# A graph-attention front in two parts: statistics of 8 tiles first, the next pair of tiles turned ahead, later edge searches moved into the first layer

## The chip, the cores and the metric

The kernel runs on one core of one Trainium2 chip. The core has five engines that run their own instruction streams and meet only at semaphores: TensorE (PE, matrix products; its weight loads are listed as PEld), VectorE (DVE), ScalarE (ACT), GpSimd (POOL) and SyncE (SP, which here only issues DMAs). The metric is the device time of one execution in microseconds (us), lower is better.

## The reference

Four blocks follow each other over 3125 nodes of 256 features, each added to x; the change touches the start of the first one.

```python
def _gat_layer(x, src, dst, W, al, ar, b, n_nodes):
    h = x @ W
    el = h @ al
    er = h @ ar
    e = jax.nn.leaky_relu(el[src] + er[dst], NEG_SLOPE)
    m = jax.ops.segment_max(e, dst, num_segments=n_nodes)
    ex = jnp.exp(e - m[dst])
    s = jax.ops.segment_sum(ex, dst, num_segments=n_nodes)
    alpha = ex / s[dst]
    out = jax.ops.segment_sum(alpha[:, None] * h[src], dst, num_segments=n_nodes)
    return out + b
...
x = x + _L0_gnn_ref(_layernorm(x), src, dst, ...)     # three such layers
x = x + _L0_ffn_ref(_layernorm(x)[None], ...)[0]      # 16 experts, 2 per node
x = x + _L1_gnn_ref(_layernorm(x), W, M, src, dst)    # relu(x@W + sum over edges of x@M)
x = x + _L1_ffn_ref(_layernorm(x)[None], ...)[0]      # 8 experts, 1 per node
```

There are 103125 edges, and the list is sorted by dst. A layer norm (mean and variance of each node's 256 features) stands ahead of the first layer.

## The kernel before

Nodes lie in 25 tiles of 128 rows (NT = 25; the last has 53). The three attention layers work on dense blocks: a count of edges for every pair of a source node and a destination node is made once, kept in SBUF as bytes (counts), and used by all layers. Destinations are taken in 13 groups of two tiles (GROUPS; the last has one).

**The front** (L984 to L1042) runs before the first layer. `load_nodes` brings x in six DMAs of 512 KB and a small one, on SP's queue. `Locator` then brings the whole list dst (whole, on ACT's queue), and copies both lists into DRAM tensors with a tail (dst_p, src_p, L1304 to L1306). `attention_weights` brings W with two extra columns (we), al and ar spread over all partitions (wa) and b (wb), and DVE makes the extra columns, W times al and W times ar, in four products (L923). `locator.find(j)` finds where the edges of part j start: DVE compares every 25th entry of dst with 98 window numbers (less, L1330), PE sums the columns in 33 small matmuls (L1336), DVE turns the sums into row numbers (at, L1338), and POOL gathers 98 rows of 400 edges from either list with indirect DMAs (L1340). There are four parts of 98 windows of 8 destinations. `locator.finish(j)` (L1352) makes the low bits and keys of these edges, with six transposes on PE and copies on ACT.

`Counter` makes the counts of 16 destinations at a time, a pair of windows; a group has 16 pairs, and there are 196 pairs. `make(pair, act)` compares iotas with the edges' low bits and keys on DVE (ohs and ohk, both L1405; with act = 2 two of the six ohs come from ACT by way of far, L1401 and L1402). `add` multiplies them in six matmuls on PE (acc_c, L1417) and ACT writes the sums to counts as bytes (L1420).

The statistics of all 25 tiles (L1009 and L1010), one Sqrt (L1014) and a reciprocal come first, with `finish(0)` between them in the text. Then comes a loop over the groups. It makes two pairs of group 0 and, for either tile, scales x to y (DVE for the first tile L1027, ACT for the second L1030), transposes y on PE (turned, L1033) and copies it to yT (L1035). `Sources.put` (L954) then multiplies yT by we in ps_m (L961), limits the two scores (lr, L964), takes two Exps (L965 and L966) and writes h (L968). Then the two pairs are added; behind groups 1 to 3 stands `find(1)` to `find(3)`.

**A layer** (L1044 on) takes the 13 groups, and for each the 25 source tiles s: DVE makes pm from tau, rho and counts (L1086; eight buffers), PE multiplies pm by h into acc (L1089). In layer 0, the pairs of the next group are made and added between these steps, about one per s. `divide` and `onward` of a group run some steps into the next group, from the list later; onward turns the result and calls `put` for the next layer. `finish(1)` to `finish(3)` stand at s = 16 of groups 1, 3 and 5. `spare_rows` gives 33 DMAs on SP that write rows for the experts, and three of them go out per group from group 2 on.

The text of the kernel isn't the order on the engines. A scheduler at build time takes instructions by their place in the text, but lets a later one go ahead where its operands are ready by its own model of times; buffers of a pool (bufs) and data decide what may pass. A small write to a tile, with another tile as its operand, is therefore used to hold an instruction back (L1008: less is copied to a statistics tile). On the chip each engine runs its stream in order.

Of the kernel before, what the change touches and what calls it, by code (L numbers as in the profile page):

```python
# [21 lines left out]
P = 128  # L22
N = 3125
NT = 25
# [882 lines left out]
LIMIT = 60.0  # L907
HELD = 64.0


def attention_weights(tc, cp, layers, i):

    nc = tc.nc
    w, al, ar, b = layers[i]
    we = cp.tile([P, KD, D + 2], F32, name="we")
    nc.sync.dma_start(we[:, :, :D], w.rearrange("(k p) f -> p k f", p=P))
    at = cp.tile([P, 2, D], F32, name="wa")
    nc.scalar.dma_start(at[:, 0], spread(al, D))
    nc.scalar.dma_start(at[:, 1], spread(ar, D))
    junk = cp.tile([P, D], F32, name="wjunk")  # L920
    for k in range(KD):
        for j in range(2):
            nc.vector.scalar_tensor_tensor(junk, we[:, k, :D], 1.0, at[:, j], op0=OP.mult, op1=OP.mult,  # L923
                                           accum_out=we[:, k, D + j:D + j + 1])
    bt = cp.tile([P, D], F32, name="wb")
    nc.scalar.dma_start(bt, spread(b, D))
    return we, bt
# [13 lines left out]
class Sources:  # L941
# [12 lines left out]
    def put(self, pp, t, r, xTs, w):  # L954
# [3 lines left out]
        for xT in xTs:  # L958
            ps = pp.tile([P, D + 2], F32, name="ps_m")
            for k in range(KD):  # L960
                nc.tensor.matmul(ps[:r], xT[:, k], w[:, k], start=(k == 0), stop=(k == KD - 1))  # L961
            pss.append(ps)
# [8 lines left out]
def dense_attention(tc, dram, counts, x_in, big, ident, eps, layers, src, dst, rows, high, make_router, over):  # L971
# [10 lines left out]
    with tc.tile_pool(name="dw", bufs=1) as cp, tc.tile_pool(name="dwl", bufs=2) as wl, \  # L982
# [5 lines left out]
        load_nodes(nc, x, x_in)  # L988
        locator = Locator(tc, cp, dram, src, dst, ident, counts)
        we, bt = attention_weights(tc, wl, layers, 0)  # L990
        now = Sources(tc, big, small)
        with tc.tile_pool(name="dp", bufs=8) as pmp, tc.tile_pool(name="ds", bufs=2) as sp, \
# [11 lines left out]
            for t in range(NT):  # L1004
                st = sp.tile([P, 6], F32, name="st")
                if t < 2:

                    nc.vector.tensor_copy(st[:NHEAD, 0:1], locator.less[:NHEAD, 0, 0:1])  # L1008
                nc.vector.bn_stats(st, x[:, t])  # L1009
                nc.vector.bn_aggr(mv[:, t], st)  # L1010
                if t == NT // 2:
                    locator.finish(0, pp)
            rstd = small.tile([P, 2, NT], F32, name="rstd")
            nc.scalar.activation(rstd[:, 0], mv[:, :, 1], AF.Sqrt, bias=eps)  # L1014
            nc.vector.reciprocal(rstd[:, 0], rstd[:, 0])
            nc.vector.scalar_tensor_tensor(rstd[:, 1], mv[:, :, 0], -1.0, rstd[:, 0], op0=OP.mult, op1=OP.mult)
            ahead = list(pairs[0])
            for a, (c, n) in enumerate(GROUPS):
                for pair in ahead[:2]:
                    counter.make(pair, 0)  # L1020
                turned = ap_.tile([P, 2, CHUNK], F32, name="acc")
                xTs = []
                for j, q in enumerate(range(0, n, P)):
                    t, r = (c + q) // P, min(P, n - q)
                    xn = sp.tile([P, D], F32, name=f"y{j}")
                    if j == 0:
                        nc.vector.tensor_scalar(xn, x[:, t], mv[:, t, 0:1], rstd[:, 0, t:t + 1], op0=OP.subtract,  # L1027
                                                op1=OP.mult)
                    else:
                        nc.scalar.activation(xn, x[:, t], AF.Identity, scale=rstd[:, 0, t:t + 1],  # L1030
                                             bias=rstd[:, 1, t:t + 1])
                    for k in range(KD):
                        nc.tensor.transpose(turned[:, j, k * P:(k + 1) * P], xn[:, k * P:(k + 1) * P], ident)  # L1033
                    xT = sp.tile([P, KD, P], F32, name="yT")
                    nc.scalar.copy(xT, turned[:, j, :D].rearrange("p (k r) -> p k r", k=KD))  # L1035
                    xTs.append(xT[:, :, :r])
                now.put(pp, c // P, min(P, n), xTs, we)
                for pair in ahead[:2]:
                    counter.add(kp, pair)
                ahead = ahead[2:]  # L1040
                if 0 < a < PARTS:
                    locator.find(a, kp)  # L1042
# [4 lines left out]
            for i in range(3):  # L1047
# [10 lines left out]
                else:  # L1058
                    nxt = Sources(tc, big, small)
                    we_n, bt = attention_weights(tc, wl, layers, i + 1)  # L1060
                for a, (c, n) in enumerate(GROUPS):
# [18 lines left out]
                    for s in range(NT):  # L1080
                        if i == 0 and s == 16 and a in (1, 3, 5):
                            locator.finish((a + 1) // 2, pp)
                        while later and later[0][0] == s:
# [16 lines left out]
                        for pair in ready:  # L1100
                            counter.make(pair, ACT_OH)
# [21 lines left out]
                    for j, (q, t, r) in enumerate(tiles if not last else []):  # L1123
                        def onward(j=j, t=t, r=r, rest=rest, nxt=nxt, w=we_n):
# [3 lines left out]
                            yT = sp.tile([P, KD, P], F32, name="yT")  # L1128
# [150 lines left out]
class Locator:  # L1279
# [8 lines left out]
    def __init__(self, tc, cp, dram, src, dst, ident, room):  # L1288
# [10 lines left out]

        none = cp.tile([1, RE], I32, name="none")  # L1300
        nc.vector.memset(none, -WIN)
        self.lists = []
        for name, of in (("dst_p", dst), ("src_p", src)):
            to = dram.tile([E + RE], I32, name=name)  # L1304
            nc.scalar.dma_start(to[:E].rearrange("(p e) -> p e", p=rows), of.rearrange("(p e) -> p e", p=rows))
            nc.scalar.dma_start(to[None, E:], none)  # L1306
            self.lists.append(to.rearrange("(t e) -> t e", e=ER))
# [18 lines left out]
        self.less = less  # L1326

        def find(j, pp):
# [10 lines left out]
            for u, of in enumerate(self.lists):  # L1339
# [12 lines left out]
    def finish(self, j, pp):  # L1352
        nc, n = self.nc, P * TW
        rel, held, low = (w[:PW] for w in self.work)
        part, high = (w[:PW] for w in self.whole)
# [206 lines left out]
```

## Time and profile before

| what | value |
|---|---|
| median of 3 runs | 2011.19 us (2011.19 to 2011.78) |
| the profiled execution | 2013.53 us, its span 2011.8 us |
| busy in the span: PE, DVE, ACT, POOL | 1899.9, 1004.2, 756.7, 287.1 us |
| L1089, the layers' matmuls | 3750, 868.1 us |
| L1405 ohk, L1417, L961 until 100 us | 28, 150 and 100 instructions |
| first L1009, L961, L1089 starts | 11.3, 48.1, 99.6 us |
| granted clock of TensorE | 0.987 over the span, 1.00 in every window until 600 us |

The span runs from the first to the last instruction of the profiled execution. A line of the order of time has a start, a duration, the engine, the line of the kernel, the operation, its output and inputs, a count where equal instructions were merged, and in brackets how long the engine had been idle before it and what released it. A table of windows gives busy time, with the number of instructions, of PE, PEld, DVE, ACT and POOL, in this order. Most small working tiles of the locator lie in the space of counts, so they carry that name.

### The profile page before, as it was taken

The page shows a single profiled execution, that of the slowest core. Times are in us where ns is not written, and L with a number is a line of the kernel's source. Part 1 is how long each engine was busy: PE and PEld are TensorE (multiplying, and loading weights), DVE is VectorE, ACT ScalarE, POOL GpSimd, SP SyncE. Part 2 cuts the span into 40 slices and gives each one's busy share as a digit, 9 for nine tenths or more (in the row PEclk, how much of TensorE's full clock was granted, in tenths as well). Part 3 has the DMA queues.
Part 4 walks back from the last instruction along what each step waited for, and adds up shares of the span by engine and source line. Part 5 has one row for each costly group of instructions (what it writes and reads, how often), then busy time and mean ns, then how long its engine had stood idle before and what let it go on. Part 6 is the DMA issues. An engine that isn't in the chain of part 4 may idle for free. (4 is left out here: it accounts for less than half of the span.)

```text
span 2011.8 us, 27108 instructions
## 1 busy us (share of the span) xinstructions
PE 1899.9 (94%) x9234; PEld 1465.1 (73%) x9234; DVE 1004.2 (50%) x2900; ACT 756.7 (38%) x2242; POOL 287.1 (14%) x398
## 2 busy tenths in 40 slices
PE   2999999999999999999999699999989999997998
PEld 1788888887888888788888356556647887554887
DVE  5888978785444444577777322122226222323222
ACT  2867867672011111122222211111116999544221
POOL 1200000000000000032222223222320000132222
PEclk9999999999999999999999799999999999998999
DMA  4001112476000000111111345545531000633664
GB/s 127 25 1 64 33 64 116 191 281 259 30 0 1 1 1 6 37 43 43 43 43 39 126 110 124 133 105 125 118 60 47 1 1 1 220 157 143 199 208 132
DMA packets 97568, 173.82 MB, mean 86 GB/s; under 512 B 9814, under 2 KB 70581, under 8 KB 97392
## 3 DMA queue, kind: packets, MB, share of 16 engines
q1 hardware_dynamic: 59292, 109.03, 15.8%
q0 software_dynamic: 17264, 35.33, 6.7%
q10 hardware_dynamic: 20866, 27.63, 4.7%
q8 instruction: 76, 1.25, 0.3%
q14 instruction: 70, 0.57, 0.1%
HBM read 82.98 MB, written 91.35 MB: 87 GB/s over the span
## 5 line engine op out<-in xcount | busy, mean ns | idle before, releaser
L1089 PE MATMUL acc<-big,pm 128*128 128x257 f32 (+1 forms) x3750 | 868.1, 382 | 2.5 <-DVE pm L1086 2.1
L1089 PEld LDWEIGHTS acc<-big,pm 128*128 128x128 f32 (+1 forms) x3750 | 681.5, 187 | 108.9 <-DVE pm L1086 7.3
L1086 DVE SCALAR_TENSOR_TENSOR pm<-tau,rho,counts 128x256 f32<-128x256 f32 (+1 forms) x975 | 432.3, 469 | 137.0 <-PE acc L1089 135.1
L715 PE MATMUL ps_h<-xsT,w 128*128 128x512 f32 x512 | 226.5, 601 | 4.0 <-ACT xsT L708 4.0
L715 PEld LDWEIGHTS ps_h<-xsT,w 128*128 128x128 f32 x512 | 96.9, 192 | 124.3 <-issue 111.8
L1206 PE MATMUL acc<-msg,cr 128*128 128x512 f32 (+1 forms) x625 | 157.8, 404 | 0.0
L1405 DVE TENSOR_TENSOR ohk<-iota_k,key 128x1200 f16<-128x1200 f16 x196 | 152.4, 778 | 2.4 <-PE acc_c L1417 2.3
L1417 PE MATMUL acc_c<-ohk,ohs 128*128 128x200 f16 x1176 | 133.3, 251 | 4.9 <-DVE ohs L1405 2.4
L1202 ACT ACTIVATE cr<-counts 128x256 fp32r<-128x256 uint8 (+1 forms) x325 | 130.5, 402 | 19.3 <-DMA sums<-y,who 11.5
L728 POOL DMA_INDIRECT sums<-y,who x64 | 99.3, 1552 | 264.3 <-DVE y L726 249.6
L1206 PEld LDWEIGHTS acc<-msg,cr 128*128 128x128 f32 (+1 forms) x625 | 114.9, 185 | 28.9 <-ACT cr L1202 1.2
L1417 PEld LDWEIGHTS <-ohs 128*128 128x128 f16 x1176 | 105.9, 99 | 29.7 <-DVE ohs L1405 4.2
L1401 ACT ACTIVATE far<-iota_s,low 128x128 f16<-128x128 f16 x360 | 123.7, 398 | 6.3 <-DVE low L1373 1.8
L868 PE MATMUL ps_y<-t_wd,hsT 128*128 x512 | 118.4, 385 | 0.0
L723 PE MATMUL ps_o<-w,hid 128*128 128x256 f32 x512 | 113.1, 379 | 0.0
L723 PEld LDWEIGHTS ps_o<-w,hid 128*128 128x128 f32 x512 | 97.3, 190 | 20.1 <-issue 7.7
L1420 ACT CAST counts<-acc_c 128x400 uint8<-128x400 f32 x196 | 94.0, 479 | 45.4 <-PE acc_c L1417 44.6
L868 PEld LDWEIGHTS ps_y<-t_wd,hsT 128*128 128x128 f32 x512 | 96.5, 194 | 12.3
L718 ACT ACTIVATE silu<-ps_h 128x512 f32<-128x512 f32 x64 | 38.2, 597 | 162.7 <-PE ps_h L715 162.7
L719 DVE TENSOR_TENSOR hid<-silu,ps_h 128x512 f32<-128x512 f32 x64 | 43.8, 688 | 104.9 <-PE ps_h L715 104.8
L777 PE MATMUL ps_H<-big,t_w 128*128 128x512 f32 (+1 forms) x224 | 93.1, 552 | 0.7 <-ACT H L779 0.5
L1071 ACT ACTIVATE tau<-ps_m 128x256 f32<-128x256 f32 (+1 forms) x39 | 14.1, 371 | 209.0 <-PE ps_m L1069 201.0
(242 smaller groups left out, 1772.0 us busy)
## 6 DMA issues: line engine op xcount, KB each, us to landing
rows<-empty SPq DMA_DIRECT2D x16, 2564.0 KB, 9.8
w<-in_L_ffn_w_dram ACTq DMA_DIRECT2D x48, 512.0 KB, 4.3
hs<-rows SPq DMA_DIRECT2D x31, 641.0 KB, 4.2
rows<-empty SPq DMA_DIRECT2D x16, 516.0 KB, 4.2
t_wd<-in_L_ffn_Wd_dram SPq DMA_DIRECT2D x8, 1024.0 KB, 10.8
xs<-rows SPq DMA_DIRECT2D x15, 516.0 KB
bias<-in_L_ffn_bd_dram SPq DMA_DIRECT2D x32, 128.0 KB
big<-in_x_dram SPq DMA_DIRECT2D x6, 512.0 KB
```

What stands on the lines that cost most here:

```text
L715: nc.tensor.matmul(ps, w[:, k, j * P:(j + 1) * P], xsT[:, k], start=(k == 0), stop=(k == KD - 1))
L723: nc.tensor.matmul(ps, hid[:, j, q * P:(q + 1) * P], o[:, j], start=(j == 0), stop=(j == nh - 1))
L728: independent(tc, f"sums{e}", nc.gpsimd.indirect_dma_start(out=sums[:, :], out_offset=bass.IndirectOffsetOnAxis(ap=who[:, q:q + 1], axis=0 ...
L868: nc.tensor.matmul(ps, hsT[:, j], d[:, ds(e, 1), j, :].rearrange("p o f -> p (o f)"), start=(j == 0), stop=(j == nh - 1))
L1086: nc.vector.scalar_tensor_tensor(pm[:, :n], tau[:, :n], now.rho[:, s:s + 1], edges[:, s, :n], op0=OP.max, op1=OP.mult)
L1089: nc.tensor.matmul(acc[:r, j, :D + 1], pm[:, q:q + r], now.h[:, s], start=(s == 0), stop=(s == NT - 1))
L1202: nc.scalar.activation(cr[:, :n], edges[:, s, :n], AF.Copy, accum_out=seen[:, a * NT + s:a * NT + s + 1])
L1206: nc.tensor.matmul(acc[:r, j].rearrange("p h d -> p (h d)"), cr[:, q:q + r], msg[:, s].rearrange("p h d -> p (h d)"), start=(s == 0), stop ...
L1401: nc.scalar.activation(far[:, i], self.iota_s, AF.Abs, scale=-1.0, bias=self.low32[:, pair, i:i + 1])
L1405: nc.vector.tensor_tensor(to[:, i:].rearrange("p t (x u) -> p t x u", u=2), iota.rearrange("p (x u) -> p x u", u=2)[:, None].to_broadcast( ...
L1417: nc.tensor.matmul(acc[:, u], ohs[:, i], ohk[:, i], start=(t == 0), stop=(t == TW - 1))
L1420: nc.scalar.copy(to[:, :, d0 % PAIR:d0 % PAIR + 2 * WIN].rearrange("p s (u d) -> p u s d", u=2), acc.rearrange("p u (s d) -> p u s d", d=WIN))
```

## The change

Eight things change.

1. `load_nodes` is followed by `attention_weights` and then by `Locator`; al, ar and W go out on ACT's queue ahead of the list, b on SP. The four products become a function that is called later. For layers 1 and 2 the loads go out on SP, behind POOL copies that read the layer's rho.
2. The list copies with a tail are made in `find(3)` alone; the other parts gather from the inputs, with the row number limited by one more DVE instruction.
3. Statistics and Sqrt come in two parts: tiles 0 to 7, and the other 17, of which six, six and five stand in groups 0 to 2.
4. 24 matmuls on less (WARM) stand on PE ahead of the first transposes; their result isn't used.
5. The second tile's y is made on POOL, from the same two operands as the first. The turn of group a + 1 stands ahead of the `put` of group a. turned and made are two PSUM tiles, each with one half for even and one for odd groups; the first tile of a `put` goes to made. yT has buffers of its own for either tile.
6. Group 0's 16 pairs are made in groups 4 to 11, two each. `finish(0)` stands in group 3, behind the last statistics.
7. `find(1)` to `find(3)` stand in layer 0, at group 0 s = 12, group 1 s = 20 and group 3 s = 12, behind that group's tau.
8. In layer 0's group 0 the far of pairs made before s = 5 is held behind tau by a POOL copy.

```diff
+WARM = 24
+FIND = [(0, 12), (1, 20), (3, 12)]
+EARLY = 8
...
+    if behind is not None:
+        for to in (we[:, 0], at[:, 0], at[:, 1], bt):
+            nc.gpsimd.tensor_copy(to[:, 0:1], behind)
+    load = (nc.scalar if behind is None else nc.sync).dma_start
+    load(at[:, 0], spread(al, D))
+    load(at[:, 1], spread(ar, D))
+    load(we[:, :, :D], w.rearrange("(k p) f -> p k f", p=P))
+    nc.sync.dma_start(bt, spread(b, D))
+
+    def products(behind=None):
+        junk = cp.tile([P, D], F32, name="wjunk")
+        if behind is not None:
+            nc.vector.tensor_copy(junk[:, 0:1], behind)
...
-            ps = pp.tile([P, D + 2], F32, name="ps_m")
+            ps = at[i] if i < len(at) else pp.tile([P, D + 2], F32, name="ps_m")
...
+            turned = ap_.tile([P, 2, CHUNK], F32, name="acc")
+            made = ap_.tile([P, 2, CHUNK], F32, name="acc")
+            for _ in range(WARM):
+                nc.tensor.matmul(turned[:PW, 0, :4 * PW], locator.less[:locator.rows, 0],
+                                 locator.less[:locator.rows, 0:4].rearrange("p q w -> p (q w)"), start=True, stop=True)
+
+            def turn(a):
+                c, n = GROUPS[a]
                 xTs = []
                 for j, q in enumerate(range(0, n, P)):
...
+                    (nc.gpsimd if j else nc.vector).tensor_scalar(xn, x[:, t], mv[:, t, 0:1], rstd[:, 0, t:t + 1],
+                                                                  op0=OP.subtract, op1=OP.mult)
+                    to = turned[:, a % 2, j * D:(j + 1) * D]
                     for k in range(KD):
+                        nc.tensor.transpose(to[:, k * P:(k + 1) * P], xn[:, k * P:(k + 1) * P], ident)
+                    xT = sp.tile([P, KD, P], F32, name=f"yT{j}")
+                    nc.scalar.copy(xT, to.rearrange("p (k r) -> p k r", k=KD))
                     xTs.append(xT[:, :, :r])
+                return xTs
+
+            statistics(0, EARLY)
+            spreads(0, EARLY)
+            xTs = turn(0)
+            products(mv[:, EARLY - 1, 0:1])
+            stats = list(range(EARLY, NT))
+            ahead = list(pairs[0])
+            for a, (c, n) in enumerate(GROUPS):
+                pairs_now = [ahead.pop(0) for _ in range(min(2, len(ahead)) if 2 * a >= EARLY else 0)]
+                for pair in pairs_now:
+                    counter.make(pair, 0)
+                while stats and len(stats) > (NT - EARLY) * (EARLY // 2 - a - 2) // (EARLY // 2 - 1):
+                    statistics(stats.pop(0), 1)
+                if 2 * a == EARLY - 2:
+                    spreads(EARLY, NT - EARLY)
+                    locator.finish(0, pp, mv[:, NT - 1, 0:1])
+                later = turn(a + 1) if a + 1 < len(GROUPS) else None
+                now.put(pp, c // P, min(P, n), xTs, we, [made[:, a % 2, :D + 2]])
+                xTs = later
+                for pair in pairs_now:
                     counter.add(kp, pair)
-                ahead = ahead[2:]
-                if 0 < a < PARTS:
-                    locator.find(a, kp)
...
+                    we_n, bt, products = attention_weights(tc, wl, layers, i + 1, now.rho[:, NT - 1:])
+                    products()
...
+                        if i == 0 and (a, s) in FIND:
+                            locator.find(FIND.index((a, s)) + 1, kp, tau[:, 0:1])
...
+                            counter.make(pair, ACT_OH, tau[:, 0:1] if a == 0 and s < 5 else None)
...
+        def find(j, pp, behind=None):
+            if behind is not None:
+                nc.vector.tensor_copy(less[:, 0, 0:1], behind)
...
+            if j < PARTS - 1:
+                nc.vector.tensor_scalar(at[:PW], at[:PW], float(NR - RE // ER), None, op0=OP.min)
+            for u, (of, name) in enumerate(self.lists):
+                if j == PARTS - 1:
+
+                    to = dram.tile([E + RE], I32, name=name)
+                    nc.sync.dma_start(to[:E].rearrange("(p e) -> p e", p=rows), of.rearrange("(p e) -> p e", p=rows))
+                    none = cp.tile([1, RE], I32, name=name)
+                    nc.gpsimd.memset(none, -WIN)
+                    nc.sync.dma_start(to[None, E:], none)
+                    of = to
...
+            if behind is not None:
+                nc.gpsimd.tensor_copy(far[:, 0, 0:1], behind)
```

`statistics(t0, n)` and `spreads(t0, n)` are the old L1003 to L1010 and L1014 to L1015 for n tiles from t0. The last line shown is in `make`; the functions called with `behind` in `finish` write three of its working tiles in the same way.

## Prediction

> **What bounds the kernel now.** I read the busy row of TensorE (PE) over the span first, then narrow windows of the first 120 us, then the order of time inside them. From the second slice of the page on PE is busy nearly without a break:
> ```profile
> PE   2999999999999999999999699999989999997998
> ```
> So the time is PE's work plus the time PE loses, and the loss sits at the start. The windows (busy us of each engine, instructions in brackets, granted clock, DMA share, GB/s):
> ```profile
> 12.00:24.00 12.00, 1.97 (x24) 1.88 (x23) 2.07 (x5) 0.00 (x0) 4.08 (x4) 1.00 0.82 239
> 24.00:36.00 12.00, 1.06 (x5) 0.79 (x6) 9.60 (x44) 3.39 (x8) 0.00 (x0) 1.00 0.16 35
> 36.00:48.00 12.00, 6.02 (x32) 4.17 (x31) 10.58 (x35) 6.23 (x15) 0.00 (x0) 1.00 0.00 0
> 48.00:60.00 12.00, 12.00 (x119) 10.63 (x118) 8.97 (x19) 8.12 (x21) 5.29 (x3) 1.00 0.09 22
> 108.00:120.00 12.00, 12.00 (x82) 10.33 (x81) 11.41 (x24) 9.82 (x28) 0.00 (x0) 1.00 0.00 0
> ```
> PE starves for 48 us and is then full. The order of time says why:
> ```profile
> 8.61 0.19 DVE L1317 TENSOR_SCALAR counts<-counts 125x33 int32<-125x33 int32 x1 [7.07 <-DMA counts<-in_dst_dram]
> 11.06 2.91 PE L1336 MATMUL acc_c<-one,counts 125*98 125x1 f16 x33 [11.06 <-DVE counts L1330]
> ...
> 26.40 0.43 DVE L923 SCALAR_TENSOR_TENSOR wjunk<-we,wa 128x256 f32<-128x256 f32 x1 [10.36 <-DMA we<-in_L_gnn_W_dram]
> ...
> 42.86 1.28 ACT L1014 ACT_TABLE_LOAD   x1
> 44.16 0.32 ACT L1014 ACTIVATE rstd<-mv,eps 128x25 f32<-128x25 f32 x1
> ...
> 48.09 2.36 PE L961 MATMUL ps_m<-we,yT 128*128 128x258 f32 x5
> ...
> 99.56 9.82 PE L1089 MATMUL acc<-big,pm 128*128 128x257 f32 x44 [0.81 <-DVE pm L1086]
> ```
> VectorE (DVE) stands for 10.36 us in front of the weights' products, since we comes last on SP's queue; behind them come the statistics of 25 tiles, the first part's finish and four pairs, so the Sqrt starts at 44.16. The first product with we starts at 48.09, layer 0 at 99.56. From there PE loses almost nothing in the layer (3.4 us of waits from 100 to 420). So I reckon one number: when the first L1089 starts, less what PE has already done by then.
>
> **When the front starts.** New ACT queue: al, ar, we, then whole. Before, whole landed at 8.54 with x beside it and two 0.4 MB copies behind it; dst_p and src_p, issued at 1.46 and 2.88, landed 8.2 and 7.9 us later. So this queue moved 1.2 MB in some 10 us; al, ar, we and whole are 0.92 MB. Whole lands at 9.5 (estimate; 8.5 if nothing delays it, 13 if 0.5 MB ahead of it costs twice its share). Then 2.45 us to the end of less (8.61 to 11.06, as before) and 2.91 for the 33 column sums: 14.9.
>
> DVE meanwhile: eight statistics at 0.41 (pitch of L1009 plus L1010), sums' reading, Sqrt 0.32, reciprocal, y: about 17; the four products 4 x 0.42: 18.5. we has landed long since, so the 10.36 us stall goes. GpSimd (POOL) issues the two edge gathers first (2.65 + 1.03 us in the trace), then its half of the turn: 20 to 21.5. PE runs the 24 WARM products in its own order ahead of the first transposes. No row has them; nearest is L1417, 0.09 us for 200 columns in a full stretch and 0.17 cold (six in 1.16), so 392 columns cost 0.18 to 0.33: 4.3 to 8 us, I take 6.1, which ends at 21. WARM is late last, not the statistics. Transposes and the copy of yT: 0.8. **First L961 at 22** (19.5 to 26), before 48.09. WARM buys warm products: the 33 sums took 2.91 us the first time and 1.64 at 51.96, though the granted clock reads 1.00 in both windows.
>
> **The groups.** Measured before: two tiles with two pairs, without a find, take 3.65 us (L961 starts at 68.18, 71.83, 75.47); with a find 4.77 (59.76, 64.53). A pair alone costs PE 0.545: the layer's step with one takes 1.41 us, without one 0.867. So a group without pairs is 2.56. The added PSUM places and the second yT let put start before the copies of the last group have read: I take 3.5 with pairs, between PE's own work (3.39) and 3.65.
> Groups 0 to 2, no pairs: DVE has six statistics, a y and two lr, 3.0 us, against PE's 2.56; DVE is 3.5 us ahead by then (18.5 against 22), so PE's time counts: 7.7. Group 3: 2.56, the six transposes of finish 0.7, and the chain of the second Sqrt (table, Sqrt, reciprocal, y, transposes, copy: 3.4 us) less the 1.9 of put it lies beside: 1.5; sum 4.8. Groups 4 to 11 with 16 pairs: 8 x 3.5 = 28. The last tile and the hand-over took 3.2 before (L961 at 96.33, L1089 at 99.56): 3.2. ACT has no part in the bound: it gives up twelve y of 0.61 us (L1030), and with two copies, two h, the Exps and two casts of counts it needs some 3.0 us of such a group's 3.5. The small additions (the min behind the sums 0.16, the marker copies on DVE 0.1 and POOL 0.25 each, as L1008 and L662) lie beside PE's work; without that cover they would be 2 us in all. Front: 22 + 7.7 + 4.8 + 28 + 3.2 = **65.7** against 99.56: 33.9 earlier.
>
> **What the front no longer did.** Before, 25 pairs were added by 99 us (150 L1417 matmuls / 6), now 16: nine more in layer 0, 9 x 0.545 = 4.9. Three finds move there too, 3 x 1.64 = 4.9 of PE, plus less (1.83 on DVE, whose 11.41 of 12 us is no cover while pairs are made): 0 to 1.5 each, taken 0.5. The DMAs of later weights now wait for rho on POOL and go out on SP; products waiting for them stop DVE, and pm behind it. Eight pm buffers are 6.9 us of PE's work, and a landing takes 4 to 8 us: 0 to 3, taken 1. The far of the first pairs waits for tau: 0 to 3, taken 1. The list copies (0.8 MB) go out on SP in group 3, two groups before finish needs them: nothing; without that cover the POOL gathers stand 8 us, with no far behind them. Layer 0 pays back 4.9 + 4.9 + 1.5 + 2 = 13.3. **Net 20.6 us.**
>
> **Two rules against it.** First, y of each second tile moves to POOL. The nearest row is L1078, 128x256 f32: 0.72 alone, 0.83 median, 2.19 at worst, beside DVE work with two inputs in SBUF. Eleven such DVE instructions beside the worst and eleven with an idle POOL:
> ```profile
> 824.75 4.91 DVE L1086 SCALAR_TENSOR_TENSOR pm<-tau,rho,counts 128x256 f32<-128x256 f32 x11
> 826.79 2.19 POOL L1078 TENSOR_TENSOR y<-y,wb 128x256 f32<-128x256 f32 x1 [3.22 <-DMA y<-in_x_dram]
> ```
> ```profile
> 99.02 4.44 DVE L1086 SCALAR_TENSOR_TENSOR pm<-tau,rho,counts 128x256 f32<-128x256 f32 x11
> ```
> DVE loses 0.47, POOL 1.4. The Trainium skill (SBUF — State Buffer, "SBUF: two separate sides") calls the shared port an exclusive lock, the loser "fully blocks": 0.83 of DVE per group. DVE needs 2.85 us in a group with pairs (two makes at 1.16, y, lr). By the row 3.3, under PE's 3.5: nothing. By the rule 3.7: 8 x 0.2 = 1.6 later. I take the row.
> Second, Sqrt now runs twice, the second time between Exps: two more table loads while PE is fed. The skill (ScalarE: Activation LUTs, "What ACT_TABLE_LOAD costs") puts a switch at 2.66 us, 1.28 and a drain, and says to batch by set. Here the load starts at 42.86 and Sqrt at 44.16: 1.30, no drain. By the row group 3 stalls 1.5; by the page, two switches, 4.2. I take the row.
>
> **Sum.** Span 2011.8 - 20.6 = 1991.2; the profiled execution was 2013.5, 1.7 more than its span, and lies 2.3 above the median of the runs, 2011.2. Forecast **1990.6**.
>
> **Rivals.** (a) A late and slow front: whole at 13, the page's table loads, the lock: 4 + 2.7 + 1.6, and 1.2 more of waits at the finds: 9.5 lost, **2000**. For it: ACT is full (11.92 of 12) from 84 to 96; against: that is far and ohs made ahead, which tau now holds back. 0.14. (b) The order of the text isn't that of the run: before, the second find's less stood at 14.23, far ahead of its place. If the other 17 statistics run ahead of the first turn, 17 x 0.41 = 7: **1997.6**. 0.12. (c) Slower: POOL can't get its operands beside back-to-back two-input makes, and PE, which has turn(a+1) ahead of put(a), stands behind it. The 12 halves decide from 5.1 us each (mean period 40.5 / 12 = 3.4, plus 20.6 / 12 = 1.7); at 6 us the kernel takes 12 x 2.6 - 20.6 = 11 more: **2022**. Against it: the worst of 25 rows is 2.19, and two y1 buffers let POOL run ahead. With order or dependencies that chain the groups to over 5 us in the same way: 0.08. (d) All lower ends: first put at 19.5, no debits: 6 more, **1984.6**. 0.07. (e) The gain is given back in layer 0: 0.04.
>
> The forecast keeps 0.55. This kernel's runs lie within 0.03%, so 0.2%, 4 us, can be told from no change. Faster 0.55 + 0.14 + 0.12 + 0.07 = 0.88; same 0.04; slower 0.08. Range 1984 to 2002: the forecast, (b), most of (a) and (d), about 0.85.
>
> **What would show it.** First L961 near 22, first L1089 near 66, no DVE wait on we; six statistics between the first turns; the POOL turn under 2.2 us; 16 pairs before L1089 and layer 0 some 10 us longer. Wrong if L961 starts after 28, if groups 4 to 11 take over 4 us each, or if DVE or POOL waits appear in layer 0 at the finds or the later weights.

## The result, and the profile after

| | before | after |
|---|---|---|
| median of 5 runs | 2011.19 us (2009.37 to 2011.78) | 2002.05 us (2001.24 to 2003.62) |
| profiled execution, its span | 2013.53, 2011.8 us | 2001.24, 1999.4 us |
| ratio after to before | | 0.9955, 95% interval 0.9944 to 0.9967 |

The change makes the kernel 9.1 us faster, 0.45%. The forecast was 20.6 us, and 2002.05 lies just outside its range. In the line numbers of the kernel after, L974 is put's product with we (before: L961), L978 and L979 the Exps, L981 h, L1025 and L1026 the statistics, L1030 the Sqrt, L1031 the reciprocal, L1037 WARM, L1046 y, L1050 the transposes, L1052 yT, L1125 the layer's product (before: L1089), L1345 the first use of the list, L1360 less, L1366 the column sums, L1413 finish's transposes.

TensorE over the span of the kernel after, in 40 slices, and the same five windows as in the prediction:

```profile
PE   5999999999999999999999699999979999997998
```

```profile
12.00:24.00 12.00, 5.16 (x41) 4.30 (x42) 5.41 (x20) 1.28 (x1) 1.23 (x2) 1.00 0.87 224
24.00:36.00 12.00, 10.08 (x52) 7.23 (x51) 11.55 (x60) 5.21 (x16) 7.29 (x10) 1.00 0.10 27
36.00:48.00 12.00, 8.49 (x40) 6.57 (x39) 7.74 (x23) 9.28 (x26) 5.00 (x4) 0.86 0.01 2
48.00:60.00 12.00, 12.00 (x89) 10.03 (x88) 10.88 (x26) 8.73 (x30) 5.49 (x4) 1.00 0.00 1
108.00:120.00 12.00, 12.00 (x78) 10.38 (x77) 12.00 (x30) 7.04 (x21) 0.00 (x0) 1.00 0.01 2
```

The first slice went from 2 to 5 tenths, one late slice from 8 to 7, and the rest is as it was. TensorE is fed from 24 us on, where before it starved until 36, and full from 48, as before; but it now does the groups in 29 to 75 us. Two things are not in the forecast: VectorE and TensorE begin the front's work only behind 16 us, and from 36 to 48, where TensorE should be full, it is busy for 8.49 of 12 at a mean clock of 0.86. In the order of time of the kernel after:

```profile
16.38 0.19 DVE L1345 TENSOR_SCALAR counts<-counts 125x33 int32<-125x33 int32 x1 [15.27 <-DMA counts<-in_dst_dram]
...
28.95 1.04 PE L974 MATMUL acc<-we,yT 128*128 128x258 f32 x4
...
35.99 1.28 ACT L1030 ACT_TABLE_LOAD   x1
37.28 0.31 ACT L1030 ACTIVATE rstd<-mv,eps 128x17 f32<-128x17 f32 x1
37.50 0.46 ACT L981 ACTIVATE big<-acc,big 128x256 f32<-128x256 f32 x1
...
38.01 1.14 PE L974 MATMUL acc<-we,yT 128*128 128x258 f32 x4 [1.55 <-ACT big L981]
...
39.79 1.28 ACT L978 ACT_TABLE_LOAD   x1
...
41.49 0.47 ACT L981 ACTIVATE big<-acc,big 128x256 f32<-128x256 f32 x1
...
42.02 1.12 PE L974 MATMUL acc<-we,yT 128*128 128x258 f32 x2 [1.22 <-ACT big L981]
...
44.33 1.66 PE L974 MATMUL ps_m<-we,yT 128*128 128x258 f32 x4
...
74.96 2.00 PE L1125 MATMUL acc<-big,pm 128*128 128x257 f32 x8 [0.85 <-DVE pm L1122]
```

The list is used at 16.4, not at 9.5; that is 7 us, and the first put is 7 us late, at 28.95. Then four groups take until 46.05, where group 4's first L974 starts: 17.1 us where 12.5 were forecast. The two waits name ScalarE's L981, the copy to h. The first time it stands behind the load of Sqrt's table and the second Sqrt, the second time behind the load that brings Exp's table back (ACT_TABLE_LOAD stands in the trace where ScalarE goes from Exp to Sqrt or back, 1.28 us each time). The four products at 44.33 took 1.66, those at 28.95 1.04. The first layer product starts at 74.96: 24.6 us before that of the kernel before, where 33.9 were forecast.

### The profile page after: what moved, and what is told of

The parts are those of the page before. It is cut to its first block, busy times and chain, and to the rows that moved or that the text cites. A ratio compares the mean times of both kernels' runs of the same rounds, so it can differ in the third digit from the quotient of the medians.

```text
span 1999.4 us, 27211 instructions
## 1 busy us (share of the span) xinstructions
PE 1901.7 (95%) x9258; PEld 1465.8 (73%) x9258; DVE 1003.3 (50%) x2909; ACT 753.0 (38%) x2232; POOL 303.1 (15%) x425
## 5 line engine op out<-in xcount | busy, mean ns | idle before, releaser
L1125 PE MATMUL acc<-big,pm 128*128 128x257 f32 (+1 forms) x3750 | 870.5, 382 | 3.0 <-DVE pm L1122 2.6
L1125 PEld LDWEIGHTS acc<-big,pm 128*128 128x128 f32 (+1 forms) x3750 | 680.7, 187 | 110.4 <-DVE pm L1122 9.0
L1452 DVE TENSOR_TENSOR ohk<-iota_k,key 128x1200 f16<-128x1200 f16 x196 | 153.1, 781 | 3.9 <-PE acc_c L1464 3.9
L1105 ACT ACTIVATE tau<-ps_m 128x256 f32<-128x256 f32 (+1 forms) x39 | 14.1, 370 | 205.5 <-PE ps_m L1103 197.5
## 6 DMA issues: line engine op xcount, KB each, us to landing
rows<-empty SPq DMA_DIRECT2D x16, 2564.0 KB, 17.8
```

Of the source, the lines that this page charges most:

```text
L1125: nc.tensor.matmul(acc[:r, j, :D + 1], pm[:, q:q + r], now.h[:, s], start=(s == 0), stop=(s == NT - 1))
L1452: nc.vector.tensor_tensor(to[:, i:].rearrange("p t (x u) -> p t x u", u=2), iota.rearrange("p (x u) -> p x u", u=2)[:, None].to_broadcast( ...
```

## The experiments

18 runs, each timed in five rounds (no_second_sqrt and half_no_sqrt in four) against the kernel before, whose medians lay between 2010.1 and 2011.5. The interval of a ratio is about 0.0028 wide, some 5.5 us, so two of these kernels that lie within 3 us can't be told apart by time; what a single edit does is read from the trace, above all from the first layer product. In the table, half clock is the time in the first 80 us of the profiled execution for which TensorE's granted clock was 0.50, and groups 0 to 3 run from the first L974 to the first L974 of group 4. As an estimate, at a clock of 0.50 such a stretch costs up to half its length, where TensorE has work all along. (Where an expectation speaks of 18.4 us, it counts to the second tile of group 4.)

| kernel | median, us | ratio to before (95%) | first L974 | groups 0 to 3 | first layer product | half clock |
|---|---|---|---|---|---|---|
| after | 2002.1 | 0.9955 (0.9944 to 0.9967) | 28.95 | 17.1 | 74.96 | 3.41 |
| list_first | 1994.8 | 0.9920 (0.9905 to 0.9934) | 20.82 | 16.9 | 66.83 | 3.41 |
| four_places | 2002.0 | 0.9950 (0.9936 to 0.9963) | 29.23 | 16.0 | 74.64 | 6.83 |
| one_sqrt | 2000.9 | 0.9952 (0.9938 to 0.9966) | 28.62 | 17.0 | 73.57 | 0 |
| all_three | 1995.5 | 0.9921 (0.9907 to 0.9935) | 21.71 | 17.8 | 66.86 | 6.83 |
| one_part | 2001.8 | 0.9954 (0.9941 to 0.9968) | 30.40 | 12.8 | 72.22 | 10.24 |
| y_dve | 1993.2 | 0.9911 (0.9897 to 0.9925) | 20.53 | 15.6 | 64.86 | 0 |
| no_warm | 1992.8 | 0.9911 (0.9897 to 0.9925) | 21.08 | 15.5 | 65.83 | 0 |
| finds_front | 1994.5 | 0.9915 (0.9901 to 0.9928) | 20.91 | 23.8 | 76.48 | 13.65 |
| fed | 1996.0 | 0.9925 (0.9912 to 0.9939) | 21.16 | 16.9 | 67.27 | 0 |
| half_stats | 1994.1 | 0.9918 (0.9904 to 0.9931) | 21.22 | 16.5 | 66.82 | 0 |
| fed_places | 1994.8 | 0.9921 (0.9907 to 0.9934) | 21.44 | 17.5 | 69.00 | 6.83 |
| fed_finds | 1996.9 | 0.9932 (0.9918 to 0.9946) | 25.01 | 20.5 | 74.47 | 6.83 |
| no_second_sqrt | 1992.4 | 0.9906 (0.9891 to 0.9921) | 21.53 | 13.8 | 64.38 | 0 |
| half_no_sqrt | 1991.0 | 0.9894 (0.9879 to 0.9909) | 21.36 | 13.8 | 64.26 | 0 |
| newton_y | 1996.3 | 0.9919 (0.9905 to 0.9932) | 20.80 | 19.0 | 68.80 | 6.83 |
| short_newton | 1995.1 | 0.9922 (0.9908 to 0.9935) | 21.40 | 16.2 | 67.84 | 3.41 |
| short_cold | 1995.1 | 0.9923 (0.9909 to 0.9936) | 21.13 | 15.0 | 65.81 | 0 |
| late_finish | 1995.0 | 0.9918 (0.9904 to 0.9931) | 20.78 | 13.2 | 65.83 | 0 |

### The list's place on its queue: list_first

```diff
-        we, bt, products = attention_weights(tc, wl, layers, 0)
         locator = Locator(tc, cp, dram, src, dst, ident, counts)
+        we, bt, products = attention_weights(tc, wl, layers, 0)
```

> Only the order on ACT's queue changes: the edge list goes out ahead of al, ar and W. Queue theory: the list waits behind 0.5 MB of small pieces on its own queue; now it lands near 8.5 instead of 16.4, the first product with we starts at 21 to 22 instead of 28.95, and the kernel takes 1995 (7 less than the changed kernel). Rival, x on the other queue takes the bandwidth: landing at 12 or later, first product at 25, 1998. Rival, the groups behind it absorb the start: 2002.

```profile
8.25 0.19 DVE L1345 TENSOR_SCALAR counts<-counts 125x33 int32<-125x33 int32 x1 [7.13 <-DMA counts<-in_dst_dram]
...
20.82 1.04 PE L974 MATMUL acc<-we,yT 128*128 128x258 f32 x4
...
66.83 2.00 PE L1125 MATMUL acc<-big,pm 128*128 128x257 f32 x8 [0.85 <-DVE pm L1122]
```

All three (list_first's order of time) come 8.1 us earlier than in the kernel after, and the median falls by 7.3. One line of order on one queue is worth almost as much as the whole change was. Groups 0 to 3 still take 16.9: the second part of the miss is another matter.

### What holds groups 0 to 3: the halves, the second Sqrt, all together

four_places gives turned and made four PSUM tiles of one bank each (and the layer's acc tiles are laid out behind them). one_sqrt makes the second part's reciprocal root by four Newton steps on VectorE, so ScalarE loads no second Sqrt table. all_three is both with list_first.

```diff
-            turned = ap_.tile([P, 2, CHUNK], F32, name="acc")
-            made = ap_.tile([P, 2, CHUNK], F32, name="acc")
+            turned = [fp.tile([P, CHUNK], F32, name=f"turned{u}") for u in range(2)]
+            made = [fp.tile([P, CHUNK], F32, name=f"made{u}") for u in range(2)]
...
```

```diff
+                if t0:
+                    nc.vector.tensor_scalar(to[:, 1], mv[:, t0:t0 + n, 1], -0.5, 1.5, op0=OP.mult, op1=OP.add)
+                    for step in range(4):
...
+                    return
                 nc.scalar.activation(to[:, 0], mv[:, t0:t0 + n, 1], AF.Sqrt, bias=eps)
```

> turned and made become four PSUM tiles of one bank each in place of two tiles with two halves. Theory that the halves don't stand alone (the first tile of a put waits for the h of the group before, and the table loads of Exp and Sqrt lie in that chain): groups 0 to 3, from the first put to the fifth, take 13 to 14 us instead of 18.45, and the kernel 1997.5. Rival, the table loads on ACT or the statistics on DVE pace these groups by themselves: at most 1 us less, 2001.

> The second part's spreads (17 tiles) are made on DVE with 17 small instructions (a series of four Newton steps) in place of the Sqrt on ACT, so the table goes from Sqrt to Exp once. Theory that the table loads stand in the chain from put to put: two loads of 1.28 us go, groups 2 and 3 take 2.6 less in all, 1999.5. Rival, the chain is long without them, or DVE's additional 2 us take their place: 2002. If a load costs a drain as well, 5 us less: 1997.

> The three edits together. If the three causes stand one behind the other: first product at 22, groups 0 to 3 in 12 us, 7 + 4.5 + 1 less than the changed kernel: 1989.5. If the table loads matter only because of the halves, the same as the first two alone: 1990.5. If an early start only meets DVE's statistics, 1995.

In the kernel after a put starts 0.05 us after the last group's L981 has read the other half (38.01 after 37.96, 42.02 after 41.96), so the halves do chain. With four tiles that wait is gone and the first four groups start at 29.23, 31.42, 34.29 and 36.35; but the fifth waits until 45.26, and the layer starts only 0.3 earlier. one_sqrt gives 1.4, no more than its missing half-clock stretch can be worth (half of 3.41); all_three gives nothing on top of list_first. None of these was the bound alone.

### One part, y on VectorE, no warming, the searches in front

All four stand on list_first. one_part takes all 25 statistics and one Sqrt ahead of the first turn; y_dve has both y on VectorE; no_warm has WARM = 0; finds_front puts the three searches back behind groups 1 to 3.

```diff
-            statistics(0, EARLY)
-            spreads(0, EARLY)
+            statistics(0, NT)
+            spreads(0, NT)
...
-            stats = list(range(EARLY, NT))
+            stats = []
...
-                    spreads(EARLY, NT - EARLY)
```

```diff
-                    (nc.gpsimd if j else nc.vector).tensor_scalar(xn, x[:, t], mv[:, t, 0:1], rstd[:, 0, t:t + 1],
+                    nc.vector.tensor_scalar(xn, x[:, t], mv[:, t, 0:1], rstd[:, 0, t:t + 1],
```

```diff
-FIND = [(0, 12), (1, 20), (3, 12)]
+FIND = []
...
+                if 0 < a < PARTS:
+                    locator.find(a, kp)
```

> On the kernel with the list's copy first (1994.8): all 25 statistics and one Sqrt ahead of the first turn, finish(0) and the pairs where they were. Theory (VectorE's work, 25 statistics at 0.56, finish(0) and the first pairs, sets when the fifth group's product starts, wherever it is cut): the first L974 7 to 9 us later, near 28.5, but four groups then take 10 to 12 instead of 18.4, the fifth starts at 39 to 41, first layer product within 2 us of 66.8, time 1994 to 1997. Rival (the two parts are what brings the gain, each group waits for the one before it): groups 0 to 3 keep some 15 to 18 us behind the later start, first layer product at 72 to 75, time 2000 to 2003.

> On the kernel with the list's copy first (1994.8): the second y of each group on VectorE in place of GpSimd. By the rows (GpSimd beside two-input work on VectorE costs VectorE 0.47 us at worst): twelve y at 0.4 us are added to VectorE, groups 4 to 11 go from 3.35 to 3.4 to 3.5 and groups 0 to 3 are 1 to 2 us later: 1996 to 1998. By the rule (an exclusive lock, 0.83 us of VectorE lost in each group): taking GpSimd away gives VectorE more than the 0.4 that it takes on: 1990 to 1994.

> On the kernel with the list's copy first (1994.8): no warming products. If they buy a warm TensorE for the first group, as the prediction held: first L974 at about the same 20.8 or 0.5 earlier, its products at twice 0.26 us each for the first 3 to 4 us, first layer product 1 to 3 us later, 1996 to 1998. If VectorE paces groups 0 to 3, the cold products lie beside its work and cost nothing: first layer product within 0.7 of 66.8, 1994 to 1995.5.

> On the kernel with the list's copy first (1994.8): the searches of parts 1 to 3 back in the front, behind groups 1, 2 and 3. Layer 0 gets the forecast 6.4 us back (3 x 1.64 of column sums, 3 x 0.5 of less). If the front pays the same (work of TensorE moved, 3 x 1.64, less beside it): first layer product 5 us later, time 1993.5 to 1996. If VectorE paces groups 0 to 3, less (3 x 1.84) adds to the column sums there: first layer product 7 to 11 us later, 1997 to 2000.

**one_part** meets the rival: the layer starts 5.4 us later and the median is 7.0 higher, so the two parts do bring something, though how much is blurred: its half-clock stretch is 6.8 us longer, and the profiled execution is the fastest of its five (1996.56). But its groups 0 to 3 take 12.8 us instead of 16.9, about what the forecast gave them: where neither statistics nor a Sqrt stand between them, they go faster. That points to VectorE or to ScalarE.

**y_dve** comes out on the side of the rule of the lock (1993.2), but not by its mechanism. As the prediction applied it, the lock would show in the makes with their two inputs (L1452). From 34 to 60 us in list_first, with GpSimd's y among them, fifteen ohk took 0.770 to 0.875 us with a median of 0.777; in y_dve, without, sixteen took 0.774 to 0.784 with a median of 0.778. One of them lost 0.1 us, and no lock is seen. It is GpSimd that slows down, from 1.24 us beside the statistics to 1.97 beside makes that keep their time (list_first's lines):

```profile
18.71 3.73 POOL L1046 TENSOR_SCALAR y<-big,mv,rstd 128x256 f32<-128x256 f32 x3 [0.24 <-DVE rstd L1031]
23.34 1.24 POOL L1046 TENSOR_SCALAR y<-big,mv,rstd 128x256 f32<-128x256 f32 x1 [0.90 <-PE acc L1050]
...
39.06 0.77 DVE L1452 TENSOR_TENSOR ohk<-iota_k,key 128x1200 f16<-128x1200 f16 x1
39.34 1.97 POOL L1046 TENSOR_SCALAR y<-big,mv,rstd 128x256 f32<-128x256 f32 x1 [4.77 <-PE acc L1050]
39.75 0.55 DVE L1452 TENSOR_TENSOR ohs<-iota_s,low 128x768 f16<-128x768 f16 x1
...
40.83 0.78 DVE L1452 TENSOR_TENSOR ohk<-iota_k,key 128x1200 f16<-128x1200 f16 x1
```

What GpSimd costs is its own time, 1.24 us for a y that VectorE makes in 0.38 to 0.41. From group 4 to the layer the two kernels need nearly the same, 29.1 and 28.8 us. Of the 2.0 us that y_dve gains at the first layer product, up to 1.7 can go with the half-clock stretch that it doesn't have, so the share of GpSimd itself is not settled.

**no_warm** isn't slower: 1.0 us earlier at the first layer product, 2.0 less in the median, which is within what can't be told apart. **finds_front** costs the front 9.7 us, of which 13.65 us at half the clock can be up to 6.8, and gives layer 0 7.2 us back (its length to the next layer's first transposes falls from 421.3 to 414.1). The net is nothing that can be measured: moving the searches brought this kernel nothing.

### The three together, and VectorE's load halved

fed is list_first with y_dve's and no_warm's edits. half_stats leaves out eight of the statistics, as its expectation says; fed_places and fed_finds add four_places with one_sqrt, and finds_front.

```diff
+                    if t >= EARLY and t % 2:
+                        nc.vector.tensor_copy(mv[:, t], mv[:, t - 1])
+                        continue
```

> The list's copy first, both y of a group on VectorE, no warming products. If what each brought alone adds up (first layer product 2.0 us earlier with y on VectorE, 1.0 without the warming, both without a stretch at half the granted clock): first layer product at 63.8 to 65, time 1990 to 1992.5. If both did nothing but spare the kernel the half-clock stretch, which lies at 34 to 38 us with the list first: first layer product 64.9 to 66, no better than either alone, 1992.5 to 1993.5.

> As fed, but the statistics of the odd tiles from tile 9 on are left out (a copy of the neighbour's mean and variance stands for them; eight tiles), so VectorE has 8 x (0.56 - 0.15) = 3.3 us less to do between the first and the fifth group and nothing else changes. Theory (VectorE's work paces groups 0 to 3): the fifth group's product and the first layer product come 2.5 to 3.5 us earlier than in fed. Rival (the chain through ScalarE and TensorE's own order, or the granted clock, sets it): less than 1 us earlier.

> As fed, with four PSUM places of one bank each and the second spread without the Sqrt (17 short VectorE instructions, some 3 us). If dependencies through the halves and the second table switch hold groups 0 to 3: first layer product 1.5 to 3 us earlier than in fed, time 1988 to 1990. If VectorE paces them, its 3 us more eat that: within 1 us of fed or later.

> As fed, with the three searches back in the front. With the list first the front then ran 13.5 us at half the granted clock, which cost it 6.7 us. If the column sums lie in TensorE's idle time where VectorE paces and the clock stays full: first layer product 2 to 4 us later than in fed and layer 0 6.4 to 8 us shorter, so 3 to 5 us faster than fed, 1986 to 1989. If VectorE's less (3 x 1.84) adds in full: 5.5 us later and 6.4 to 8 shorter, 0 to 2.5 faster. If the clock falls again: fed plus 2 to 4.

fed missed both expectations: it is no faster than either edit alone, and its layer starts later (67.27). Without warming its first eight products are slow until 26 us (four took 1.93 us where list_first's took 1.04); and TensorE's waits for yT are 3.9 us where y_dve has 1.0. **half_stats** decides: 3.3 us less on VectorE bring 0.45 at the first layer product. VectorE, though busy for 12.6 of the 14 us from 20 to 34, doesn't pace these groups in fed. fed_places is later than fed, and fed_finds is 7.2 later in front and 4.8 shorter in layer 0.

### ScalarE's order: no_second_sqrt and half_no_sqrt

no_second_sqrt is fed without the Sqrt and the reciprocal of the second part; half_no_sqrt leaves out half_stats' eight statistics too.

```diff
+                if t0:
+                    nc.vector.tensor_copy(to[:, 0], mv[:, t0:t0 + n, 1])
+                    return
                 nc.scalar.activation(to[:, 0], mv[:, t0:t0 + n, 1], AF.Sqrt, bias=eps)
```

> As fed, with the Sqrt and the reciprocal of the second part left out (a copy of the variance stands for them), so ScalarE loads Exp once and no table after it: 2 x 1.28 + 0.31 = 2.9 us less on ScalarE, nothing else moved. If ScalarE's order (yT copies queued behind the loads) sets groups 0 to 3: first layer product 2 to 3 us earlier than fed's 67.3, so 64.3 to 65.3. If VectorE's work or TensorE's sets it: less than 0.7 earlier.

> As no_second_sqrt, with the statistics of eight tiles left out too (3.3 us of VectorE). If ScalarE's order is the bound: within 0.7 us of no_second_sqrt, as half_stats was of fed. If the two engines take turns, each hidden by the other: first layer product 2 to 3 us earlier again, 61.5 to 63. If neither counts: within 1 us of fed's 67.3.

ScalarE in the order of time, in fed and then in no_second_sqrt (where the copy to yT is L1055):

```profile
26.57 1.28 ACT L978 ACT_TABLE_LOAD   x1
...
28.06 0.35 ACT L1052 COPY yT<-acc 128x256 f32<-128x256 f32 x1
...
29.18 1.28 ACT L1030 ACT_TABLE_LOAD   x1
30.47 0.31 ACT L1030 ACTIVATE rstd<-mv,eps 128x17 f32<-128x17 f32 x1
30.80 1.28 ACT L978 ACT_TABLE_LOAD   x1
...
32.30 0.35 ACT L1052 COPY yT<-acc 128x256 f32<-128x256 f32 x1
```

```profile
25.93 1.28 ACT L978 ACT_TABLE_LOAD   x1
...
27.43 0.35 ACT L1055 COPY yT<-acc 128x256 f32<-128x256 f32 x1
...
29.39 0.37 ACT L1055 COPY yT<-acc 128x256 f32<-128x256 f32 x1 [0.86 <-PE acc L974]
```

In fed one yT ends at 28.4 and the next starts at 32.30: between them stand two copies to h, the Sqrt's table, the Sqrt, Exp's table and two Exps, in one stream, and TensorE's next transposes need the place that this yT frees. Without the switch the same step takes from 27.8 to 29.39. Groups 0 to 3 fall from 16.9 to 13.8, and the first layer product comes 2.9 us earlier, at 64.38. half_no_sqrt adds 0.1. So in fed it is ScalarE's order, not a turn of the two engines.

### In place of the switch: newton_y, short_newton, short_cold, late_finish

newton_y is y_dve with one_sqrt's steps; short_newton takes two Newton steps (which serve only a variance near 1) and holds finish behind them; short_cold has no warming; late_finish puts finish and the pairs one group later.

```diff
-                    locator.finish(0, pp, mv[:, NT - 1, 0:1])
+                    locator.finish(0, pp, rstd[:, 0, NT - 1:])
```

```diff
-                pairs_now = [ahead.pop(0) for _ in range(min(2, len(ahead)) if 2 * a >= EARLY else 0)]
+                pairs_now = [ahead.pop(0) for _ in range(min(2, len(ahead)) if 2 * a > EARLY else 0)]
...
                 later = turn(a + 1) if a + 1 < len(GROUPS) else None
+                if 2 * a == EARLY:
+                    locator.finish(0, pp, rstd[:, 0, NT - 1:])
```

> The list's copy first, both y on VectorE, warming kept, and the second spread by 17 short VectorE instructions in place of the second Sqrt (2.9 us less on ScalarE, 3.0 more on VectorE). Against y_dve (first layer product at 64.9, 1993.2): if ScalarE's order is the bound, 1.5 to 2.5 us earlier, 1990.5 to 1992; if VectorE takes over, as in the kernel with all three changes, 0 to 2 us later, 1993 to 1995.

> As y_dve (the list's copy first, both y on VectorE, warming kept), the second spread by 9 short VectorE instructions (some 1.5 us) that run ahead of finish(0), in place of the second Sqrt. If the length of the chain on VectorE was what ate the gain in newton_y: first layer product 1 to 2.5 us before y_dve's 64.9, no stretch at half the granted clock in the front, time 1990 to 1992. If TensorE idles as long as before and falls to half the clock: at 66 to 69 again, 1994 to 1997.

> As short_newton without the warming products. If they are worth the cold products of the first groups only (in fed the first sixteen L974 took some 0.42 us each in place of 0.26): first layer product 1.5 to 2.5 us later than in short_newton. If the warming is what makes TensorE fall to half the clock later: no later, and no such stretch here.

> As short_newton, with finish(0) behind the turn of group 5 and group 0's pairs in groups 5 to 12. If finish ahead of the turn in TensorE's queue is what is left of the wait in groups 0 to 3: no stretch at half the granted clock, first layer product 62.5 to 64.5, time 1989 to 1992. If the pairs, now squeezed towards the end, take its place: 65 to 68, 1993 to 1996.

All four land at 1995 to 1996, no better than list_first. TensorE's waits from 28 to 42 us in newton_y:

```profile
PE ps_m L1421 <- DVE rstd L1035: 1.8, 1, 1.8
PE acc L974 <- DVE counts L1410: 1.1, 1, 1.1
```

L1421 there is finish's transposes: they stand in TensorE's queue ahead of the fifth group's turn and wait for finish's work on VectorE, which the Newton steps now delay. With that moved (late_finish) groups 0 to 3 take 13.2 us, near the 12.5 of the forecast; but the pairs, made one group later, follow more slowly: from group 4 to the layer it takes 31.9 us, where list_first takes 29.1, and the layer starts at 65.83. I read this as several chains of nearly the same length, where each one shortened leaves the next as the bound; no single run shows that.

The lowest medians of kernels that leave nothing out are no_warm's 1992.8, y_dve's 1993.2 and finds_front's 1994.5, with list_first and fed_places at 1994.8, all under both given kernels; among these the runs don't tell.

## Why the prediction was wrong

| term of the sum | forecast | after |
|---|---|---|
| list lands | 9.5 (8.5 to 13) | 16.4 |
| list to first put | 12.5 | 12.6 |
| groups 0 to 3 | 12.5 | 17.1 |
| groups 4 to 11 | 28 | 26.4 (to the last tile's product at 72.45) |
| last tile, hand-over | 3.2 | 2.5 |
| layer 0 pays back | 13.3 | 14.1 (405.5 to 419.6) |
| rest | 0 | 1.9 less |
| profile over median | 2.3 above | 0.8 below |

**The first step that failed** is "So this queue moved 1.2 MB in some 10 us; al, ar, we and whole are 0.92 MB. Whole lands at 9.5". It took a queue's end for bytes over a rate. The list, issued 2.5 us into the span behind three other transfers, was used 13.9 us after its issue; issued first, at 0.81, 7.4 us after. So the list was used 6.9 us later than forecast, and list_first shows that the order on the queue was the cause: with it alone changed, everything comes 8.1 us earlier. My upper bound of 13 was a guess at twice the share, and the real value lay beyond it. The rival (a) had a late list with that bound, and its 2000 came closest in time, though in part by luck: the lock that it added did not appear, and of its waits at the finds 0.6 us did.

**The second** is "DVE is 3.5 us ahead by then (18.5 against 22), so PE's time counts: 7.7", with 4.8 for group 3. The count asked of TensorE and VectorE which is later, and said that ScalarE "has no part in the bound", from its load in a group with pairs. Ahead of the pairs ScalarE has less to do but carries the table switches, and the copies to h and to yT, which TensorE waits for, stand behind them. (The 3.5 us were off too: VectorE's last product ended at 27.9, 1.0 us ahead of the first put.) The groups took 4.6 us more than forecast. On fed the second Sqrt with its two loads is worth 3.1; 1.5 of that was in the forecast, so 1.6 is missing from it, if the switch costs the kernel after as much as fed. The half-clock stretch in the kernel after costs about 1.7: L974 in pairs at 42.02 and 43.42 took 1.12 for 0.70, L1413 0.70 for 0.42 and four L974 1.66 for 1.04. These are 3.3 of the 4.6. The other 1.3 stay open: in the kernel after TensorE waits there for yT (1.2 us), for GpSimd's y (0.7) and for VectorE (0.5), and no run takes these apart.

Of the two rules weighed, "ScalarE: Activation LUTs" of the Trainium skill was right in its advice to batch by set (Table sets: the hidden batching unit), and 2.66 us a switch (What ACT_TABLE_LOAD costs) was too dear here. The loads took 1.28 to 1.30 with no drain to be seen, as I took from the row; but I charged 1.5 for the switch pair, an estimate from the page's figure would have made it 4.2 with my working, and it measured 2.9 to 3.1, about the loads and the Sqrt themselves (2 x 1.28 + 0.31): they were simply not hidden. The lock of "SBUF — State Buffer" (SBUF: two separate sides) isn't seen on the makes in list_first, whose times agree with y_dve's, and rival (c) never came near.

**What held**: the 12.5 us from list to first put, in part by luck. WARM's length was right (5.9 against 6.1), but VectorE's statistics and y, forecast 4 us ahead of its end, ended with it: the first transposes waited for VectorE's y until 27.74, WARM ended at 27.5, and no_warm's first put is no earlier. Further, groups 4 to 11 were full of TensorE's own work, at 3.3 a group instead of 3.5, and the debit of layer 0 came within 0.8, with the searches' share measured at 7.2 and 4.8 us against 6.4. That the searches gained nothing by the move doesn't show in the sum, because it stood on both sides of it. Rival (b) didn't happen: of the other 17 statistics three ran ahead of the first y, eight between VectorE's first four y (two, four and two, where the forecast had six each time) and six behind them. The one wait for later weights was 0.9 us. TensorE waited 1.4 us for the first pair's ohs, where 1 was allowed for far, and 1.1 us at the counts' copy, which wasn't forecast.

The last 3.1 us of the miss in the median are the profile's own place among the runs: before's execution lay 2.3 above its median, after's 0.8 below. I carried the first over.

## What to carry to other kernels

Ask of every transfer that the first work waits for what is issued ahead of it on the same queue, and put it first: a figure of bytes over a mean rate hides the order, and here the order was worth 7 us. In a start-up stage list all engines in order, the small ones too: a table load on an engine that is idle for 62% of the span stops whatever stands behind it in that one stream. Where several chains of nearly the same length meet, single edits can show nothing; leave work out on one engine at a time to learn which of them is the bound before you rebuild it.

## What the runs showed of the hardware

The granted clock falls for whole stretches. Every half-clock stretch in the front is a multiple of 3.41 us: 3.41, 6.83, 10.24 and 13.65 in the table above. That is the window of 4096 cycles (3413 ns) that the Trainium skill gives in "TensorE: Matmul & The Clock Gate" (Part 1: The HAM clock gate). Windows of the kernel after (clock third from the end), then of finds_front:

```profile
38.00:40.00 2.00, 1.61 (x9) 1.26 (x9) 1.93 (x6) 1.57 (x5) 1.76 (x1) 1.00 0.00 0
40.00:42.00 2.00, 0.44 (x2) 0.20 (x2) 0.06 (x1) 1.99 (x6) 2.00 (x3) 1.00 0.00 0
42.00:44.00 2.00, 1.98 (x7) 1.60 (x8) 0.72 (x2) 1.38 (x6) 0.71 (x1) 0.54 0.00 0
44.00:46.00 2.00, 2.00 (x8) 1.57 (x7) 1.32 (x3) 0.74 (x3) 0.00 (x0) 0.60 0.02 4
```

```profile
38.00:42.00 4.00, 4.00 (x36) 3.56 (x34) 1.70 (x5) 1.36 (x5) 3.64 (x3) 0.50 0.23 67
42.00:46.00 4.00, 4.00 (x18) 3.34 (x18) 2.55 (x7) 1.72 (x7) 2.75 (x3) 0.50 0.19 53
```

The clock fell in the kernel after without an idle gap of TensorE over 1.55 us in the groups before it. The page's rule is no idle gaps over some 3.4 us, though it also tells of a kernel whose short idle times set the clock swinging. In finds_front the clock stayed at half through 8 us in which the profile shows TensorE busy, where the page has one busy window release it. So the profile's busy time doesn't tell here when the clock changes. Executions of one kernel differ by up to 7.7 us (one_part: 1996.56 to 2004.24); that the place of these windows causes it wasn't tried.

The clock's row doesn't show a slow start. In fed, without warming, four L974 took 1.93 us, in list_first 1.04, and the row reads 1.00 in fed all the while:

```profile
23.73 1.93 PE L974 MATMUL ps_m<-we,yT 128*128 128x258 f32 x4
```

```profile
22.00:24.00 2.00, 2.00 (x8) 1.65 (x8) 1.85 (x9) 0.40 (x2) 0.00 (x0) 1.00 0.04 15
```
